# A sparse graph-attention stack: weighted rows in buffers of their own, one-head sums on VectorE

## The chip, the cores and the metric

The kernel runs on one core of one Trainium2 chip. A core has five engines [...]: TensorE (PE, matrix products into PSUM), VectorE (DVE), ScalarE (ACT), GpSimd (POOL, which here issues the gathers and scatters) and SyncE (SP, which issues plain transfers). [...] The metric is the device time of one execution in microseconds (us); it is given as the median of several runs, and the profile is one more execution taken by the hardware profiler.

## The reference, cut to what matters

Four graph-attention layers, each with a layer norm and a ReLU ahead and a residual around it, on 3327 nodes with 512 features. The layers have 8, 4, 1 and 8 heads; layers 1 and 2 end in an ELU.

```python
h = relu(layernorm(x)); v = h @ W                  # 3327 x 512
e[i, j] = leaky_relu(a[i] + b[j], 0.2)             # per head, masked by the adjacency
alpha = softmax(e, axis=j)
out[i] = sum over j of alpha[i, j] * v[j]          # per head
x = x + elu(out)                                   # without elu in layers 0 and 3
```

The adjacency is sparse: a node has 36 neighbours at most, itself included.

## The kernel before: the parts that matter

A first stage (to about 395 us) reads the adjacency, makes for each node a list of its neighbours, sorts the nodes by their number and cuts them into 26 tiles of 128 nodes. Tile t has `CAPS[t]` neighbour places per node, from 36 down to 11, 467 in all. Then each layer runs over the tiles, smallest first, in groups of up to four neighbour places (127 groups). For one place, one gather brings 128 rows of the table `tab` (a projected row of 512 values with its scores, 528 in all), one for each node of the tile.

```python
LOOK = 9
gpool = tile_pool(name="gpool", bufs=LOOK)         # a buffer g holds one group: [128, 4, 528]
...
def fetch(self):                                   # GpSimd: gathers of one group
    g = gpool.tile([P, GROUP, ROW], F32, name="g")
    for q in range(n):
        if l > 0 and k0 + q == 0:
            nc.sync.dma_start(g[:, 0, :], own_d[l % 2][t])        # the node's own row
        else:
            gather(g[:, q, :], tabs[l % 2], idx[:, t, k0 + q:k0 + q + 1])      # L677
...
def scored(self, i):                               # weights of one group
    nc.vector.tensor_tensor(z, g's scores, s, OP.add)                           # L721
    nc.vector.scalar_tensor_tensor(z, z, SLOPE, z, OP.mult, OP.max)             # L723
    nc.scalar.activation(self.wt[:, k0:k0 + n, :H], z, AF.Exp)                  # L724
...
def group(self, i):                                # weight the rows in place, sum them
    for q in range(n):
        v = g[:, q, :] ... [:, :, :F // 2]         # the 512 values, as 2 x 256
        if H == 1:
            nc.scalar.activation(v, v, AF.Copy, scale=wt[:, k0 + q, 0:1])       # L734
        elif q == 3:
            for h in range(H):                     # one activation a head
                nc.scalar.activation(u, u, AF.Copy, scale=wt[:, k0 + q, h:h + 1])  # L738
        else:
            nc.vector.tensor_tensor(v, v, wt broadcast over the head, OP.mult)  # L741
    for q in range(n):                             # sum in PSUM, by the identity
        nc.tensor.matmul(self.po, ident, g[:, q] ..., start=..., stop=...)      # L744
```

When a tile's groups are done, its tail follows in pieces:

```python
def divisors(self):  ...                           # VectorE: 1 / sum of the weights (L750-752)
def means(self):     y = po * den                  # VectorE reads TensorE's sums (L758)
def bent(self):      ...                           # ScalarE, ELU layers only: exp part (L766, L768)
def added(self):     x += y (or its ELU)           # VectorE (L774, L775 or L777), then layer-norm
                     ...                           # statistics and 1/sqrt by Newton steps (L411-L434)
def turn(self):      ...                           # TensorE: four transposes (L444)
def cut(self):       ...                           # ScalarE: ReLU, PSUM to SBUF (L451)
def project(self):   ...                           # TensorE: 8 matmuls with the next W (L462)
def rows(self):      ...                           # ScalarE: scale (L469); SP stores the own rows
def scatter():       ...                           # GpSimd: rows into the next layer's tab (L685)
```

The order of instructions on each engine is that of this loop. Step s fetches groups ahead, scores group s+1, weights and sums group s, and lays the tail's pieces into the following steps:

```python
for s in range(-1, len(steps) + 6):
    while fetched < min(len(steps), s + LOOK): fetch the next group
    do("first"); score group s + 1; do("scored"); weight and sum group s
    if it was the tile's last group:
        late = 1 if ELU[l] else 0
        for d, place, piece in [(0, "last", tl.divisors), (1, "last", tl.means),
                                (2, "scored", tl.bent), (1 + late, "last", tl.added),
                                (2 + late, "first", tl.turn), (2 + late, "scored", tl.cut),
                                (2 + late, "last", tl.project), (3 + late, "scored", tl.rows),
                                (3 + late, "last", scatter)]:
            at.setdefault((s + d, place), []).append(piece)
    do("last")
```

A buffer can be written again when its last reader is done; a gather into g waits for the engine that read g last. Layer l+1 starts gathering when all tiles of layer l are scattered.

Of the kernel before, what the change touches and what calls it, by code (L numbers as in the profile page):

```python
# [20 lines left out]
HEADS = [8, 4, 1, 8]  # L21
SELF = [True, True, False, False]
ELU = [False, True, True, False]
BANK = 512
# [9 lines left out]
GROUP = 4  # L34
# [439 lines left out]
def tile_gat_stack(ctx: ExitStack, tc: tile.TileContext, x, adj, adjT, ws, avs, out):  # L474
# [173 lines left out]
    with cond.Else():  # L648
        tile_gat_lists(tc, x, ws, avs, out, ident, half, idx, tabs, tabs_v)
# [3 lines left out]
def tile_gat_lists(ctx: ExitStack, tc: tile.TileContext, x, ws, avs, out, ident, half, idx, tabs, tabs_v):  # L653

    nc = tc.nc
    NP, F = x.shape
    NT = NP // P
    NL = len(HEADS)

    LOOK = 9  # L660
    xpool = ctx.enter_context(tc.tile_pool(name="xpool", bufs=1))
    wpool = ctx.enter_context(tc.tile_pool(name="wpool", bufs=2))
    gpool = ctx.enter_context(tc.tile_pool(name="gpool", bufs=LOOK))
    spool = ctx.enter_context(tc.tile_pool(name="spool", bufs=3))
# [17 lines left out]
    def scatter():  # L682
        while waiting:
            dst, t, rows = waiting.pop(0)
            nc.gpsimd.indirect_dma_start(out=dst, out_offset=bass.IndirectOffsetOnAxis(ap=ids[t], axis=0),  # L685
                                         in_=rows, in_offset=None)

    class Tile:
# [22 lines left out]
        def scored(self, i):  # L711

            H = HEADS[self.l]
            k0, n, g = self.groups[i]
            if i == 0:
                self.s = small.tile([P, 8], F32, name="s")
                nc.vector.tensor_copy(self.s[:, :H], g[:, 0, F // 2:F // 2 + H])
                self.wt = spool.tile([P, KMAX, 8], F32, name="wt")
                self.po = ps_o.tile([P, BANK], F32, name="po")
            z = small.tile([P, GROUP, 8], F32, name="z")  # L720
            nc.vector.tensor_tensor(z[:, :n, :H], g[:, :n, ROW - 8:ROW - 8 + H],  # L721
                                    self.s[:, :H].unsqueeze(1).to_broadcast([P, n, H]), OP.add)
            nc.vector.scalar_tensor_tensor(z[:, :n, :H], z[:, :n, :H], SLOPE, z[:, :n, :H], OP.mult, OP.max)  # L723
            nc.scalar.activation(self.wt[:, k0:k0 + n, :H], z[:, :n, :H], AF.Exp)  # L724

        def group(self, i):

            H, K, wt = HEADS[self.l], CAPS[self.t], self.wt
            D = F // H
            k0, n, g = self.groups[i]  # L730
            for q in range(n):
                v = g[:, q, :].rearrange("p (s m) -> p s m", s=2)[:, :, :F // 2]
                if H == 1:
                    nc.scalar.activation(v, v, AF.Copy, scale=wt[:, k0 + q, 0:1])  # L734
                elif q == 3:
                    for h in range(H):
                        u = v[:, h * 2 // H, h * D % (F // 2):h * D % (F // 2) + D]
                        nc.scalar.activation(u, u, AF.Copy, scale=wt[:, k0 + q, h:h + 1])  # L738
                else:
                    v = v.rearrange("p s (h d) -> p s h d", d=D)  # L740
                    nc.vector.tensor_tensor(v, v, wt[:, k0 + q, :H].rearrange("p (s h) -> p s h", s=2)  # L741
                                            .unsqueeze(3).to_broadcast([P, 2, H // 2, D]), OP.mult)
            for q in range(n):
                nc.tensor.matmul(self.po, ident, g[:, q, :].rearrange("p (s m) -> p s m", s=2)[:, :, :F // 2],  # L744
                                 start=(k0 + q == 0), stop=(k0 + q == K - 1))

        def divisors(self):
            H, K = HEADS[self.l], CAPS[self.t]
# [3 lines left out]
            nc.vector.reciprocal(den[:, :H], den[:, :H])  # L752

        def means(self):
            H, po, den = HEADS[self.l], self.po, self.den
            D = F // H
            self.y = work.tile([P, F], F32, name="y")
            nc.vector.tensor_tensor(self.y.rearrange("p (h d) -> p h d", h=H),  # L758
                                    po.rearrange("p (h d) -> p h d", h=H),
                                    den[:, :H].unsqueeze(2).to_broadcast([P, H, D]), OP.mult)  # L760

        def bent(self):
# [45 lines left out]
    for l in range(NL):  # L808
        W, following = following, None
        tiles = [Tile(l, t, W) for t in order]  # L810
        steps = [(tl, i) for tl in tiles for i in range(len(tl.k0))]
        at = {}
        fetched = 0
        for s in range(-1, len(steps) + 6):
            def do(place):
                for piece in at.pop((s, place), []):
                    piece()
            while fetched < min(len(steps), s + LOOK):
                steps[fetched][0].fetch()
# [65 lines left out]
```

## Time and profile before

| | |
|---|---|
| time, median of 3 runs | 3442.64 us (3437.56 to 3452.84) |
| profiled execution | 3448.7 us |
| busy: PE, DVE, ACT, POOL | 2380.0, 1690.1, 1111.7, 1990.4 us |
| gathers of rows (L677) | 1790, 1003 ns each |
| products on VectorE (L741) | 1080, 686 ns each |
| weighting by ScalarE in layer 2 (L734) | 467, 712 ns each |
| data moved | 628.25 MB, 182 GB/s on average |

A line of the page's groups names the source line, the engine, the operation, the tile written and those read, the shape, and the count; then the busy time, the mean length of one, and the engine's idle time just before these instructions with what ended most of it. "issue" is idle time for which the profile shows no wait. One matmul of four-byte values shows as two records. GpSimd's record of a gather is the time of its instruction; the data lands after it. The granted clock is the share of full speed that TensorE's throttle let through.

### The profile page before, as it was taken

To read this page: it belongs to the slowest core of one execution; us is meant where nothing else is said; L and a number is where in the kernel's file an instruction comes from. 1 tells how busy PE (TensorE), PEld (TensorE's weight loads), DVE (VectorE), ACT (ScalarE), POOL (GpSimd) and SP (SyncE) were. 2 spreads that over 40 slices of the span, in tenths; PEclk is the share of its full clock that TensorE was granted. 3 is DMA by queue.
4 is the path that set the end of the run, shared out by engine and by line. 5 is a ranking of instruction groups with operands and counts; after the bars stand their busy time and mean duration, and the time that the engine had idled before them with its cause. 6 is when DMAs were issued, how large, how long until landed. Compare 5 with 4: busy or idle time off the path is not lost.

```text
span 3448.7 us, 26822 instructions
## 1 busy us (share of the span) xinstructions
PE 2380.0 (69%) x5830; PEld 1182.6 (34%) x5830; DVE 1690.1 (49%) x4748; ACT 1111.7 (32%) x3431; POOL 1990.4 (58%) x2027
## 2 busy tenths in 40 slices
PE   4554157777777767887777667777777756775766
PEld 2443033333333324443333333333333322332322
DVE  9999246555545446665554323222212145453544
ACT  0111023243333323232322244454454423332433
POOL 1002667666667367676666366556556267777775
PEclk7777578988888879998988889898898878887898
DMA  5552466666666567776666466566666376777675
GB/s 210 205 190 88 126 189 195 200 191 192 189 184 192 138 191 211 199 208 191 197 192 177 117 199 186 171 184 184 177 183 190 88 203 199 204 199 202 197 202 144
DMA packets 197017, 628.25 MB, mean 182 GB/s; under 512 B 38483, under 2 KB 42995, under 8 KB 193525
## 3 DMA queue, kind: packets, MB, share of 16 engines
q0 software_dynamic: 154432, 519.29, 53.7%
q1 hardware_dynamic: 38676, 100.36, 8.4%
q10 hardware_dynamic: 3744, 6.82, 0.5%
q8 instruction: 54, 0.88, 0.1%
q14 instruction: 111, 0.90, 0.1%
HBM read 569.76 MB, written 56.57 MB: 182 GB/s over the span
## 4 chain that ended last, share of the span: by engine, by line
issue 14%; PE 12%; POOL 12%; another core or an unknown queue 11%; DVE 9%; DMA 3%; ACT 3%; POOLq 0%; DVEq 0%; ACTq 0%
POOL g L677 12%; PE po L744 10%; DVE g L741 4%; DMA g<-tab,idx 3%; PE pv L462 2%; ACT g L734 1%; ACT g L738 1%; DVE st L411 1%; DVE x L775 1%; DVE q L432 1%; DVE x L774 1%; DVE z L721 1%; DVE xn L415 1%; POOL tab L685 0%
## 5 line engine op out<-in xcount | busy, mean ns | idle before, releaser
L744 PE MATMUL po<-g,ident 128*128 128x512 f32 x3736 | 1874.0, 658 | 802.3 <-ACT g L738 171.3
L677 POOL DMA_INDIRECT g<-tab,idx x1790 | 1794.7, 1003 | 844.2 <-issue 490.3
L744 PEld LDWEIGHTS po<-g,ident 128*128 128x128 f32 x3736 | 765.1, 210 | 1821.0 <-issue 976.9
L741 DVE TENSOR_TENSOR g<-g,wt 128x512 f32<-128x512 f32 x1080 | 683.1, 686 | 373.9 <-ACT wt L724 217.5
L738 ACT ACTIVATE g<-g,wt 128x64 f32<-128x64 f32 (+1 forms) x2140 | 574.4, 347 | 90.0 <-issue 57.0
L462 PE MATMUL pv<-w,hT 128*128 128x264 f32 x1664 | 458.7, 436 | 26.4 <-ACT hT L451 22.6
L758 DVE TENSOR_TENSOR y<-po,den 128x512 f32<-128x512 f32 x104 | 72.0, 692 | 823.8 <-PE po L744 508.0
L724 ACT ACTIVATE wt<-z 128x32 f32<-128x32 f32 (+7 forms) x508 | 107.7, 215 | 1116.1 <-DVE z L723 360.6
L462 PEld LDWEIGHTS pv<-w,hT 128*128 128x128 f32 x1664 | 360.4, 219 | 146.1 <-issue 36.3
L469 ACT ACTIVATE v<-pv,rstd 128x528 f32<-128x528 f32 x104 | 72.9, 701 | 835.5 <-remote 377.5
L734 ACT ACTIVATE g<-g,wt 128x512 f32<-128x512 f32 x467 | 298.4, 712 | 0.0
L685 POOL DMA_INDIRECT tab<-v,idx x78 | 80.8, 1036 | 241.3 <-ACT v L469 212.7
L444 PE MATMUL pt<-ident,xn 128*128 128x128 f32 x416 | 72.8, 304 | 168.3 <-DVE xn L415 110.8
L721 DVE TENSOR_TENSOR z<-g,s 128x32 f32<-128x32 f32 (+7 forms) x508 | 92.5, 182 | 183.0 <-DMA g<-tab,idx 163.0
L425 POOL TENSOR_TENSOR rstd<-ve,half 128x1 f32<-128x1 f32 x26 | 14.3, 552 | 290.5 <-DVE ve L417 280.4
L451 ACT ACTIVATE hT<-pt 128x512 f32<-128x512 f32 x104 | 61.2, 589 | 245.0 <-PE pt L444 106.3
L546 DVE MAX8 cand<-key 128x8 f32<-128x208 f32 x416 | 135.2, 405 | 0.0
L444 PEld LDWEIGHTS pt<-ident,xn 128*128 128x128 f32 x416 | 54.3, 154 | 223.0 <-issue 149.3
L723 DVE SCALAR_TENSOR_TENSOR z<-z 128x32 f32<-128x32 f32 (+7 forms) x508 | 92.8, 183 | 34.8 <-remote 9.5
L750 DVE TENSOR_REDUCE den<-wt 128x8 f32<-128x120 f32 (+35 forms) x104 | 32.7, 314 | 155.4 <-ACT wt L724 139.3
L541 DVE SCALAR_TENSOR_TENSOR key<-a,keys 128x3328 f32<-128x3328 int32 x26 | 94.5, 3633 | 0.0
L432 DVE TENSOR_SCALAR q<-rstd,hv 128x1 f32<-128x1 f32 x234 | 63.9, 273 | 13.3 <-issue 1.9
(82 smaller groups left out, 759.0 us busy)
## 6 DMA issues: line engine op xcount, KB each, us to landing
a<-in_adj SPq DMA_DIRECT2D x26, 1664.0 KB
g<-tab,idx POOLq DMA_INDIRECT x1790
own<-v SPq DMA_DIRECT2D x78, 264.0 KB
g<-own SPq DMA_DIRECT2D x78, 264.0 KB
tab<-v SPq DMA_DIRECT2D x26, 264.0 KB
xt<-in_x ACTq DMA_DIRECT2D x26, 256.0 KB
w<-in_w SPq DMA_DIRECT2D x8, 512.0 KB
av<-in_a SPq DMA_DIRECT2D x8, 256.0 KB
```

Of the source, the lines that this page charges most:

```text
L432: nc.vector.tensor_scalar(q, rstd, rstd, hv, OP.mult, OP.mult)
L444: nc.tensor.transpose(pt[:, k, :], xn[:, k * P:(k + 1) * P], ident)
L462: nc.tensor.matmul(pv[:, s, :HF + 8], hT[:, k, :], W.w[:, k, s, :], start=(k == 0), stop=(k == KC - 1))
L541: nc.vector.scalar_tensor_tensor(key, a, 0.0, keys, OP.is_gt, OP.mult, accum_out=total[:, t:t + 1])
L546: nc.vector.max(cand[:, g * 8:(g + 1) * 8], key[:, g * SEG:(g + 1) * SEG])
L677: nc.gpsimd.indirect_dma_start(out=out_, out_offset=None, in_=table, in_offset=bass.IndirectOffsetOnAxis(ap=which, axis=0))
L721: nc.vector.tensor_tensor(z[:, :n, :H], g[:, :n, ROW - 8:ROW - 8 + H], self.s[:, :H].unsqueeze(1).to_broadcast([P, n, H]), OP.add)
L724: nc.scalar.activation(self.wt[:, k0:k0 + n, :H], z[:, :n, :H], AF.Exp)
L734: nc.scalar.activation(v, v, AF.Copy, scale=wt[:, k0 + q, 0:1])
L738: nc.scalar.activation(u, u, AF.Copy, scale=wt[:, k0 + q, h:h + 1])
L741: nc.vector.tensor_tensor(v, v, wt[:, k0 + q, :H].rearrange("p (s h) -> p s h", s=2) .unsqueeze(3).to_broadcast([P, 2, H // 2, D]), OP.mult)
L744: nc.tensor.matmul(self.po, ident, g[:, q, :].rearrange("p (s m) -> p s m", s=2)[:, :, :F // 2], start=(k0 + q == 0), stop=(k0 + q == K - 1))
```

## The change

It has four parts, meant to let the engines run past each other:

- the weighted rows of a group go into a buffer m of their own (3 of them), so that a gather buffer is free as soon as it has been weighted; the gathers look 7 instead of 9 groups ahead, which makes room for m;
- in the layer with one head, TensorE and ScalarE no longer weight and sum the rows: VectorE multiplies each row by its weight and adds it to one of two alternating accumulators in SBUF, in one instruction a row;
- the means read TensorE's result two groups after the tile's last group instead of one (with one head, one group after, from the accumulators);
- the later pieces of the tail move back as well: the transposes one step after the residual, the projection one step after those, the rows and the scatter two steps after the projection.

```diff
-    LOOK = 9
+    LOOK = 7
+    apool = ctx.enter_context(tc.tile_pool(name="apool", bufs=2))
+    mpool = ctx.enter_context(tc.tile_pool(name="mpool", bufs=3))
...
-                self.po = ps_o.tile([P, BANK], F32, name="po")
+                if H > 1:
+                    self.po = ps_o.tile([P, BANK], F32, name="po")
... group():
+            if H == 1:
+                if i == 0:
+                    self.acc = apool.tile([P, 2, F], F32, name="acc")
+                for q in range(n):
+                    v = g[:, q, :].rearrange("p (s m) -> p s m", s=2)[:, :, :F // 2]
+                    acc = self.acc[:, (k0 + q) % 2, :].rearrange("p (s m) -> p s m", s=2)
+                    w = wt[:, k0 + q, 0:1]
+                    if k0 + q < 2:
+                        nc.vector.tensor_scalar(acc, v, w, None, OP.mult)
+                    else:
+                        nc.vector.scalar_tensor_tensor(acc, v, w, acc, OP.mult, OP.add)
+                return
+            m = mpool.tile([P, GROUP, F], F32, name="m")
             for q in range(n):
-                if H == 1:
-                    nc.scalar.activation(v, v, AF.Copy, scale=wt[:, k0 + q, 0:1])
-                elif q == 3:
+                if q == 3:
                     for h in range(H):
-                        nc.scalar.activation(u, u, AF.Copy, scale=wt[:, k0 + q, h:h + 1])
+                        nc.scalar.activation(m[:, q, h * D:(h + 1) * D], u, AF.Copy, scale=wt[:, k0 + q, h:h + 1])
                 else:
-                    nc.vector.tensor_tensor(v, v, wt ..., OP.mult)
+                    nc.vector.tensor_tensor(m[:, q, :] ..., v ..., wt ..., OP.mult)
             for q in range(n):
-                nc.tensor.matmul(self.po, ident, g[:, q, :] ..., start=(k0 + q == 0), stop=(k0 + q == K - 1))
+                nc.tensor.matmul(self.po, ident, m[:, q, :], start=(k0 + q == 0), stop=(k0 + q == K - 1))
... means():
+            if H == 1:
+                nc.vector.tensor_add(self.y, self.acc[:, 0, :], self.acc[:, 1, :])
+                nc.vector.tensor_scalar(self.y, self.y, den[:, 0:1], None, OP.mult)
+                return
... the loop:
-        for s in range(-1, len(steps) + 6):
+        for s in range(-1, len(steps) + 9):
-                    late = 1 if ELU[l] else 0
-                    for d, place, piece in [(0, "last", tl.divisors), (1, "last", tl.means),
-                                            (2, "scored", tl.bent), (1 + late, "last", tl.added),
-                                            (2 + late, "first", tl.turn), (2 + late, "scored", tl.cut),
-                                            (2 + late, "last", tl.project), (3 + late, "scored", tl.rows),
-                                            (3 + late, "last", scatter)]:
+                    a = 1 if HEADS[l] == 1 else 2
+                    b = a + 1 if ELU[l] else a
+                    for d, place, piece in [(0, "last", tl.divisors), (a, "last", tl.means),
+                                            (a + 1, "scored", tl.bent), (b, "last", tl.added),
+                                            (b + 1, "first", tl.turn), (b + 2, "scored", tl.cut),
+                                            (b + 2, "last", tl.project), (b + 4, "scored", tl.rows),
+                                            (b + 4, "last", scatter)]:
```

More of the change, by code (lines that the diff above doesn't have):

```diff
@@ L730, in group @@
             k0, n, g = self.groups[i]
+            if H == 1:
[11 more added lines that the diff above has]
+            m = mpool.tile([P, GROUP, F], F32, name="m")
             for q in range(n):
                 v = g[:, q, :].rearrange("p (s m) -> p s m", s=2)[:, :, :F // 2]
-                if H == 1:
-                    nc.scalar.activation(v, v, AF.Copy, scale=wt[:, k0 + q, 0:1])
-                elif q == 3:
+                if q == 3:
                     for h in range(H):
                         u = v[:, h * 2 // H, h * D % (F // 2):h * D % (F // 2) + D]
-                        nc.scalar.activation(u, u, AF.Copy, scale=wt[:, k0 + q, h:h + 1])
+                        nc.scalar.activation(m[:, q, h * D:(h + 1) * D], u, AF.Copy, scale=wt[:, k0 + q, h:h + 1])
                 else:
-                    v = v.rearrange("p s (h d) -> p s h d", d=D)
-                    nc.vector.tensor_tensor(v, v, wt[:, k0 + q, :H].rearrange("p (s h) -> p s h", s=2)
+                    nc.vector.tensor_tensor(m[:, q, :].rearrange("p (s h d) -> p s h d", s=2, d=D),
+                                            v.rearrange("p s (h d) -> p s h d", d=D),
+                                            wt[:, k0 + q, :H].rearrange("p (s h) -> p s h", s=2)
                                             .unsqueeze(3).to_broadcast([P, 2, H // 2, D]), OP.mult)
             for q in range(n):
-                nc.tensor.matmul(self.po, ident, g[:, q, :].rearrange("p (s m) -> p s m", s=2)[:, :, :F // 2],
-                                 start=(k0 + q == 0), stop=(k0 + q == K - 1))
+                nc.tensor.matmul(self.po, ident, m[:, q, :], start=(k0 + q == 0), stop=(k0 + q == K - 1))
         def divisors(self):
@@ L754, in means @@
         def means(self):
-            H, po, den = HEADS[self.l], self.po, self.den
+            H, den = HEADS[self.l], self.den
             D = F // H
             self.y = work.tile([P, F], F32, name="y")
+            if H == 1:
+                nc.vector.tensor_add(self.y, self.acc[:, 0, :], self.acc[:, 1, :])
+                nc.vector.tensor_scalar(self.y, self.y, den[:, 0:1], None, OP.mult)
+                return
             nc.vector.tensor_tensor(self.y.rearrange("p (h d) -> p h d", h=H),
-                                    po.rearrange("p (h d) -> p h d", h=H),
+                                    self.po.rearrange("p (h d) -> p h d", h=H),
                                     den[:, :H].unsqueeze(2).to_broadcast([P, H, D]), OP.mult)
```

## The prediction

> **What bounds the kernel now.** I read the page's busy line first: no engine is full (PE 69%, POOL 58%, DVE 49%, ACT 32% of 3448.7 us). So waits matter, and the next question is who waits for whom. The page's costliest groups (line, engine, operation, tile, count | busy us, mean ns | idle before it and what ended most of it):
>
> ```profile
> L744 PE MATMUL po<-g,ident 128*128 128x512 f32 x3736 | 1874.0, 658 | 802.3 <-ACT g L738 171.3
> L677 POOL DMA_INDIRECT g<-tab,idx x1790 | 1794.7, 1003 | 844.2 <-issue 490.3
> ...
> L758 DVE TENSOR_TENSOR y<-po,den 128x512 f32<-128x512 f32 x104 | 72.0, 692 | 823.8 <-PE po L744 508.0
> ```
>
> The third is the striking one: VectorE stands idle 824 us in front of only 104 instructions, the `means`, mostly until TensorE has finished a tile's sums. The view of waits repeats it and adds that GpSimd's gathers wait for TensorE too, to release a buffer:
>
> ```profile
> DVE y L758 <- PE po L744: 508.0, 74, 23.5
> ...
> POOL g L677 <- PE po L744: 208.5, 96, 11.1
> ```
>
> One tile end in the timeline (start us, length us, engine, line; in brackets the idle time before) shows the ring:
>
> ```profile
> 1000.30 0.95 POOL L677 DMA_INDIRECT g<-tab,idx  x1 [2.78 <-PE po L744]
> ...
> 1004.36 0.69 DVE L758 TENSOR_TENSOR y<-po,den 128x512 f32<-128x512 f32 x1 [5.22 <-PE po L744]
> ...
> 1009.52 1.89 DVE L741 TENSOR_TENSOR g<-g,wt 128x512 f32<-128x512 f32 x3
> 1009.62 1.41 POOL L677 DMA_INDIRECT g<-tab,idx  x1 [0.30 <-DMA g<-tab,idx]
> 1009.64 0.23 ACT L724 ACTIVATE wt<-z 128x32 f32<-128x32 f32 x1 [10.14 <-DVE q L432]
> ...
> 1010.26 5.40 PE L744 MATMUL po<-g,ident 128*128 128x512 f32 x8 [2.08 <-DVE g L741]
> ```
>
> VectorE waits 5.22 us for TensorE; then it does the residual, the statistics and the Newton steps before the next weights and products (1004.36 to 1009.52), and TensorE runs dry behind it. Each engine runs in order, so the two alternate instead of overlapping. Meanwhile a row block is free for the next gather only when TensorE has read it, because it is weighted in place.
>
> The third view is busy time by window, one for each layer's gathers (us of the window, then PE, PEld, DVE, ACT, POOL busy with counts, granted clock, DMA share, GB/s):
>
> ```profile
> 395.00:1160.20 765.20, 559.83 (x1380) 274.01 (x1381) 408.74 (x1076) 241.62 (x972) 525.29 (x517) 0.85 0.68 194
> 1203.00:1899.50 696.50, 522.82 (x1346) 262.62 (x1347) 395.89 (x1056) 193.36 (x613) 463.66 (x457) 0.88 0.69 196
> 1959.40:2690.60 731.20, 525.34 (x1328) 260.38 (x1329) 175.45 (x700) 337.81 (x646) 433.76 (x449) 0.87 0.64 184
> 2763.80:3420.00 656.20, 449.15 (x900) 185.45 (x900) 311.66 (x751) 234.51 (x951) 470.88 (x462) 0.83 0.70 199
> ```
>
> GpSimd's own floor follows from it. When it isn't held, the timeline shows 0.30 us between gathers. A layer has 467 neighbour rows (sum of CAPS); layer 0 gathers all of them and 26 tiles of x, later layers 441 (26 own rows come through SP), and 25 scatters fall inside. With busy/count of the window plus 0.30:
> - layer 0: 518 x (1.016 + 0.30) = 682 us; first to last gather took 766.
> - layer 1: 466 x 1.315 = 613; took 708 (1202.9 to 1910.6).
> - layer 2: 466 x 1.266 = 590; took 752 (1958.1 to 2709.8).
> - layer 3: 466 x 1.319 = 615; took about 660.
>
> So 84 + 95 + 162 + 45 = 386 us are waits of GpSimd inside the layers. TensorE is lower: a matmul record every 0.43 us in the timeline, so a tile of 18 rows costs 36 x 0.43 + 3.7 (projection) + 0.6 (transposes) = 19.8 us against about 23.7 for GpSimd's 18 instructions at 1.315. Between layers GpSimd also stops for the tail:
>
> ```profile
> 1195.11 0.98 POOL L685 DMA_INDIRECT tab<-v,idx  x1 [32.39 <-ACT v L469]
> 1202.93 0.98 POOL L677 DMA_INDIRECT g<-tab,idx  x1 [6.84 <-issue]
> ```
>
> [...]
> - [...] The trace has 692 for `means` and 693 for the existing multiply-adds of 128x512 (L775). I price the new multiply-add with that.
> - [...] counted over all gathers of rows by overlap of start and length, 708 that met no VectorE instruction mean 949 ns and none is over 1000, while 604 that met an L741 product mean 1082 ns; the 1.41 us gather above started 0.1 us into one.
> - [...]
>
> **The change part by part.**
> 1. *Means one step later* (several heads: two groups after the last instead of one). VectorE asks for TensorE's result when TensorE has had one more group's time, 8 x 0.43 = 3.4 us of matmul work stands between, and while VectorE does its 5 us tail TensorE still has two groups to sum. It removes no work, but the 508 us of VectorE waiting and TensorE's drought after each tile. Turn, cut, project and rows also get one step more each.
> 2. *Weighted rows in m (3 buffers), LOOK 9 to 7.* A gather buffer is free after the multiply, not after the matmul; the 208.5 us should nearly vanish. Lookahead falls from 8 groups to 6, still about 6 x 4 x 1.315 = 31 us of gathers, against a VectorE tail of about 7 us. Products cost the same 686 ns.
> 3. *Layer 2 on VectorE.* It removes 467 activations at 712 ns (ScalarE) and 934 matmul records (402 us at 0.43). It adds 467 x 0.69 = 322 us on VectorE plus 26 x (0.69 + 0.55) for adding the two accumulators and dividing, while a 0.69 us `means` goes. VectorE's layer 2: 322 + 46 (127 groups of two z operations at 0.18) + 126 (26 tails of 4.84: two ELU adds, statistics, Newton) + 12 (divisors) + 32 (means) + 15 (own scores, folding) = 553 us.
>    With VectorE that full I let 80% of the gathers meet a two-input operation: 0.8 x 1.08 + 0.2 x 0.95 = 1.055; 441 x 1.355 + 25 x 1.3 = 630 us, 40 more than its floor now. VectorE stands at 553/630 = 88%.
>
> If the waits go, GpSimd sets the pace. The first tiles are the exception: with 11 rows GpSimd needs 10 x 1.315 + 1.3 = 14.4 us, TensorE 22 x 0.43 + 4.3 = 13.8 at full clock, VectorE in layer 2 about 15.4. I add 12 us each for layers 0 and 1, 15 for layer 2 and 10 for layer 3, an allowance. Layers: 694 + 625 + 645 + 625 = 2589.
> Between layers: now 41, 48 and 54 us. At the first one the last matmul ends about 23 us after the last gather, since GpSimd was far ahead; 11 more to the scatter, 8 to the next gather. Consumers close behind GpSimd should need about 12 in place of the 23, with the ELU's extra about 33: 3 x 33 = 99.
> Sum: 395 before the first gather (unchanged) + 2589 + 99 + 24 at the end (3424.9 to 3448.7) = 3107; I say 3110 us, a ratio of 0.903.
>
> **Rivals.**
> - *VectorE becomes the bound in layer 2, or starves the gathers.* For it: 88% full, in order, and gathers that start 0.1 us into a product take about 0.4 us more. If nearly every gather paid 0.25 us, layer 2 would take 441 x 1.5 + 33 = 695. Against it: GpSimd's next gather falls into step with a run of products, and many overlap at 949. Total then about 3160.
> - *The shorter lookahead gives the wait back:* GpSimd held by fewer buffers, a scatter that waits for a later `rows`. Against it: data lands fast, in a stretch of uninterrupted gathers at most two or three gathers are issued and not yet moved. If half of the 386 us stayed: about 3260.
> - *TensorE or its clock becomes the bound.* Its busy time at the granted 0.85 was 560 and 523 us in layers 0 and 1, below 682 and 613; only the small tiles come near. Worth 30 us more.
> - *The transfers are the limit.* Against it: 220 GB/s in an uninterrupted stretch (2080 to 2085) with a DMA share of 0.78, and layer 0 would need 194 x 765/694 = 214.
>
> **Range and chances.** No rival alone brings it near 3443; all waits gone and no allowance would be about 3040. 8 in 10: 3020 to 3240. Faster by over 2%: 0.95; within: 0.04; slower: 0.01.
>
> **What would show it.** Right: the wait of `means` for po under 100 us; gathers waiting for TensorE gone; first-to-last gathers near 694, 625, 645, 625; gather mean in layer 2 near 1.05 us; VectorE over 80% busy there and PE under 25%; gaps between layers near 33. Wrong: gathers that wait for VectorE or ScalarE (the new owner of the buffer) by 100 us and more, a gather mean over 1.15 in layer 2, or VectorE full there with GpSimd idle.

## The result, and the profile after

The changed kernel takes 3341.63 us (median of 4 runs, 3339.68 to 3355.12), the kernel before 3446.51 beside it: a ratio of 0.9706, 95% interval 0.9671 to 0.9741. That is faster, but by 105 us where 333 were predicted. The profiled execution took 3339.0 us.

The page of the changed kernel: the chain that ended last, by engine, and the costliest groups (columns as in the prediction):

```profile
DVE 14%; PE 11%; another core or an unknown queue 11%; issue 11%; POOL 9%; DMA 6%; ACT 2%; DVEq 0%; POOLq 0%; ACTq 0%
...
L679 POOL DMA_INDIRECT g<-tab,idx x1790 | 1829.7, 1022 | 743.1 <-issue 501.3
L760 PE MATMUL po<-m,ident 128*128 128x512 f32 x2802 | 1383.5, 648 | 582.2 <-issue 215.3
L755 DVE TENSOR_TENSOR m<-g,wt 128x512 f32<-128x512 f32 x1080 | 683.6, 686 | 581.7 <-remote 371.2
...
L745 DVE SCALAR_TENSOR_TENSOR acc<-g,wt,acc 128x512 f32<-128x512 f32 x415 | 287.7, 747 | 22.8 <-DVE acc L745 11.0
...
L777 DVE TENSOR_TENSOR y<-po,den 128x512 f32<-128x512 f32 x78 | 53.7, 688 | 120.2 <-PE po L760 89.0
```

The wait of the means has gone as foreseen (824 us of idle time before them are 120 now), yet GpSimd's idle time fell only from 844 to 743 us. The idle time moved: VectorE now stands 582 us before its products, where the kernel before had 374, and the releaser is "remote", something the profile can't name. The same line of the kernel before:

```profile
L741 DVE TENSOR_TENSOR g<-g,wt 128x512 f32<-128x512 f32 x1080 | 683.1, 686 | 373.9 <-ACT wt L724 217.5
```

Waits of the changed kernel (engine, line, waited for: us in total, times, longest):

```profile
DVE m L755 <- remote: 371.2, 38, 18.1
...
ACT v L469 <- remote: 306.2, 22, 26.6
...
ACT m L753 <- remote: 164.2, 16, 17.8
ACT hT L451 <- remote: 137.1, 9, 24.8
...
POOL g L679 <- ACT m L753: 77.5, 35, 10.0
```

Gathers no longer wait for TensorE; they wait for ScalarE and VectorE, the new owners of the buffers, which themselves stand. By layer, the windows from first to last gather (us; PE, PEld, DVE, ACT, POOL busy; granted clock, DMA share, GB/s):

```profile
393.40:1160.10 766.70, 550.73 (x1393) 276.87 (x1394) 412.16 (x1087) 248.07 (x998) 524.60 (x517) 0.85 0.67 194
1197.20:1889.60 692.40, 541.86 (x1381) 268.88 (x1382) 409.50 (x1094) 204.10 (x641) 470.97 (x465) 0.88 0.69 200
1928.60:2605.00 676.40, 178.67 (x500) 130.11 (x500) 479.63 (x1208) 83.48 (x226) 491.45 (x465) 0.60 0.70 205
2636.00:3310.20 674.20, 441.01 (x902) 184.94 (x902) 311.99 (x748) 228.62 (x949) 470.27 (x465) 0.83 0.68 195
```

Against 764.9, 707.6, 751.7 and 659.8 us before, layer 2 gained 75 us and layer 1 15, layers 0 and 3 lost 2 and 14. The gaps between layers fell from 143 to 107 us in all, start and end together changed by less than 1: in sum the 109.7 between the two profiles. Counting every pause of GpSimd beyond its usual 0.30 us, its waits inside the layers went from 85, 96, 163 and 47 us to 88, 82, 46 and 65. Of these, 98 us before and 88 after stand in front of scatters, which wait for ScalarE to write the rows. So the question is why layers 0, 1 and 3 kept theirs.

**A tile end of layer 0.** The timeline of the changed kernel (start, length, engine, line; idle time before in brackets):

```profile
1072.40 2.07 PE L760 MATMUL po<-m,ident 128*128 128x512 f32 x2 [4.22 <-issue]
...
1074.27 5.76 PE L462 MATMUL pv<-w,hT 128*128 128x264 f32 x16
...
1075.47 0.23 ACT L727 ACTIVATE wt<-z 128x32 f32<-128x32 f32 x1 [1.11 <-DVE z L726]
...
1089.55 1.01 PE L760 MATMUL po<-m,ident 128*128 128x512 f32 x1 [2.22 <-issue]
...
1092.34 1.01 PE L760 MATMUL po<-m,ident 128*128 128x512 f32 x1 [1.77 <-issue]
...
1094.45 1.01 PE L760 MATMUL po<-m,ident 128*128 128x512 f32 x1 [1.10 <-issue]
...
1101.52 1.90 DVE L755 TENSOR_TENSOR m<-g,wt 128x512 f32<-128x512 f32 x3 [15.77 <-remote]
...
1102.32 0.70 ACT L469 ACTIVATE v<-pv,rstd 128x528 f32<-128x528 f32 x1 [26.62 <-remote]
...
1103.30 1.00 POOL L687 DMA_INDIRECT tab<-v,idx  x1 [6.07 <-ACT wt L727]
```

TensorE's projection is through at 1080.0 and TensorE goes on with the next sums; ScalarE, which waits for nothing but this projection, starts at 1102.3, 22 us later. GpSimd gathers on at its steady pace until it comes to the scatter of these very rows, which starts at 1103.30, 0.28 us after ScalarE has written them. VectorE's 15.77 us are a late start too: its next product writes the m buffer that TensorE had last read by 1074.47 (first line), and its weights were ready at 1075.70. TensorE's own matmuls meanwhile come only every 2.1 to 2.8 us, and the profile shows no wait for it. Then everything starts at once. In the trace, 10 updates of the semaphore on which TensorE counts its finished work lie between 1101.4 and 1102.6, the last nine 0.04 to 0.06 us apart; the whole trace has 1227 of them, that of the same kernel on a chip without late starts 1687. The ends of matmuls are modelled in the profile, and no record tells when a result could be read; so the trace can't say whether result or count was late. It does say that the next matmuls had started (the first at 1079.86).

I paired each such reader with its producer over the whole trace and took the start minus the later of two ends, the producer's and that of the reader's own preceding instruction. Over 0.3 us, summed (us):

| reader <- producer | before | changed |
|---|---|---|
| ScalarE hT <- TensorE transposes (78) | 105 | 152 |
| ScalarE v <- TensorE projection (78) | 225 | 287 |
| VectorE y <- TensorE sums (104; 78) | 241 | 71 |
| ScalarE weights <- VectorE z (508) | 14 | 17 |
| TensorE projection <- ScalarE hT (78) | 0 | 0 |
| TensorE transposes <- VectorE xn (78) | 1 | 4 |

In these six pairs late starts, up to 22 us, are found practically only where something waits for TensorE. The table is not complete, though. Counted in the same way, the changed kernel's products start late after everything they need, TensorE's last read of their m buffer included: VectorE's by 475 us in all (227 of it in layer 3), ScalarE's by 193 (all in layer 3). The m buffers themselves made this handover. VectorE also starts late on its own results: between instructions that only need the one before (accumulations, statistics, Newton steps and the like) there are 104 us of pauses, 82 of them in layer 2. In the kernel before, VectorE's products start 56 us late after ScalarE's weights. On chip B (below), where the six pairs have no late start, all of these together are one pause of 0.46 us. So late starts are not confined to TensorE's results.

The profile before had them too. In its view of waits they stand among the lines that the prediction quotes, between the 508.0 and the 208.5 us. Its chain that ended last, and these waits:

```profile
issue 14%; PE 12%; POOL 12%; another core or an unknown queue 11%; DVE 9%; DMA 3%; ACT 3%; POOLq 0%; DVEq 0%; ACTq 0%
```

```profile
ACT v L469 <- remote: 377.5, 32, 17.0
...
DVE y L758 <- remote: 241.7, 17, 21.4
```

A one-core program has no other core to wait for; 11% of the chain under that name is 380 us.

### The profile page after: what moved, and what is told of

It is laid out like the page before. It is cut to its first block, busy times and chain, and to the rows that moved or that the text cites. A ratio compares the mean times of both kernels' runs of the same rounds, so it can differ in the third digit from the quotient of the medians.

```text
span 3339.0 us, 23138 instructions
## 1 busy us (share of the span) xinstructions
PE 1968.0 (59%) x4896; PEld 1030.7 (31%) x4896; DVE 1995.3 (60%) x5241; ACT 828.7 (25%) x2964; POOL 2026.2 (61%) x2027
## 4 chain that ended last, share of the span: by engine, by line
DVE 14%; PE 11%; another core or an unknown queue 11%; issue 11%; POOL 9%; DMA 6%; ACT 2%; DVEq 0%; POOLq 0%; ACTq 0%
PE po L760 9%; POOL g L679 9%; DMA g<-tab,idx 5%; DVE m L755 4%; DVE acc L745 3%; PE pv L462 2%; ACT m L753 1%; DVE z L724 1%; DVE q L432 1%; DVE st L411 1%; DVE x L794 1%; DVE x L793 1%; DVE z L726 1%; DVE rstd L434 1%
## 5 line engine op out<-in xcount | busy, mean ns | idle before, releaser
L679 POOL DMA_INDIRECT g<-tab,idx x1790 | 1829.7, 1022 | 743.1 <-issue 501.3
L760 PE MATMUL po<-m,ident 128*128 128x512 f32 x2802 | 1383.5, 648 | 582.2 <-issue 215.3
L755 DVE TENSOR_TENSOR m<-g,wt 128x512 f32<-128x512 f32 x1080 | 683.6, 686 | 581.7 <-remote 371.2
L760 PEld LDWEIGHTS po<-m,ident 128*128 128x128 f32 x2802 | 568.0, 208 | 1327.2 <-issue 803.3
L462 PE MATMUL pv<-w,hT 128*128 128x264 f32 x1664 | 524.2, 482 | 232.0 <-ACT hT L451 173.2
L753 ACT ACTIVATE m<-g,wt 128x64 f32<-128x64 f32 (+1 forms) x2140 | 565.0, 345 | 205.9 <-remote 164.2
L462 PEld LDWEIGHTS pv<-w,hT 128*128 128x128 f32 x1664 | 401.7, 246 | 369.3 <-ACT hT L451 191.2
L745 DVE SCALAR_TENSOR_TENSOR acc<-g,wt,acc 128x512 f32<-128x512 f32 x415 | 287.7, 747 | 22.8 <-DVE acc L745 11.0
L777 DVE TENSOR_TENSOR y<-po,den 128x512 f32<-128x512 f32 x78 | 53.7, 688 | 120.2 <-PE po L760 89.0
L793 DVE SCALAR_TENSOR_TENSOR x<-ex,x 128x512 f32<-128x512 f32 x52 | 35.9, 691 | 135.2 <-ACT ex L787 113.6
```

What stands on the lines that cost most here:

```text
L462: nc.tensor.matmul(pv[:, s, :HF + 8], hT[:, k, :], W.w[:, k, s, :], start=(k == 0), stop=(k == KC - 1))
L679: nc.gpsimd.indirect_dma_start(out=out_, out_offset=None, in_=table, in_offset=bass.IndirectOffsetOnAxis(ap=which, axis=0))
L745: nc.vector.scalar_tensor_tensor(acc, v, w, acc, OP.mult, OP.add)
L753: nc.scalar.activation(m[:, q, h * D:(h + 1) * D], u, AF.Copy, scale=wt[:, k0 + q, h:h + 1])
L755: nc.vector.tensor_tensor(m[:, q, :].rearrange("p (s h d) -> p s h d", s=2, d=D), v.rearrange("p s (h d) -> p s h d", d=D), wt[:, k0 + q, ...
L760: nc.tensor.matmul(self.po, ident, m[:, q, :], start=(k0 + q == 0), stop=(k0 + q == K - 1))
```

## The experiments

The theory at the start: TensorE's results reach their readers late as long as gathers run unbroken. Rival A, from the prediction: the shorter lookahead gives the waits back. Rival B: TensorE is the bound. The runs were placed on five chips, called A to E here; each is compared with the kernel before on the same chip.

| run | chip | us | before there | ratio, 95% interval |
|---|---|---|---|---|
| later reading alone | A | 3027.05 | 3040.02 | 0.9962 (0.9948 to 0.9976) |
| one-head part alone | A | 3068.08 | 3040.02 | 1.0098 (1.0081 to 1.0115) |
| m buffers, LOOK 7 alone | A | 3051.50 | 3040.02 | 1.0038 (1.0024 to 1.0053) |
| changed kernel, LOOK 5 | A | 3072.97 | 3040.02 | 1.0109 (1.0092 to 1.0126) |
| kernel before | B | 3039.87 | 3039.62 | one execution |
| changed kernel | B | 3065.02 | 3039.62 | 1.0092 (1.0075 to 1.0109) |
| changed, layer 2 undone | B | 3022.56 | 3039.62 | 0.9939 (0.9920 to 0.9958) |
| one-head part, again | C | 3060.41 | 3036.98 | 1.0081 (1.0055 to 1.0107) |
| later reading, again | C | 3020.08 | 3036.98 | 0.9940 (0.9918 to 0.9961) |

The kernel before takes 3037 to 3040 us on A, B and C, 3448 and 3441 on D and E, and 3443 in the first runs, whose chip the records don't name. The chip is the great variable of this case.

**Parts alone (chip A).** Later reading, in place, 9 groups ahead:

```diff
-                    late = 1 if ELU[l] else 0
-                    for d, place, piece in [(0, "last", tl.divisors), (1, "last", tl.means), ...
+                    a = 2
+                    b = a + 1 if ELU[l] else a
+                    for d, place, piece in [(0, "last", tl.divisors), (a, "last", tl.means), ... as in the change
```

> The kernel before with only the later reading (means two groups after the tile's last group in all four layers, transposes, projection, rows and scatter later as in the change); rows still weighted in place, 9 groups ahead, layer 2 still on ScalarE and TensorE. Theory (TensorE's results reach their waiters late, 5 to 20 us after TensorE is done, as long as gathers run unbroken, so the engines stop all the same until the gathers have run out of buffers): the wait of the means for po falls from 508 us to under 200, but the waits of ScalarE and VectorE labelled remote grow, and the time falls by 0 to 50 us only. Rival A (the lookahead of 7 groups gives the wait back): with 9 groups kept, this part alone brings 80 us and more. Rival B (TensorE is the bound of layers 0, 1 and 3): within 20 us of the kernel before.

The one-head layer on VectorE, all else as before:

```diff
+            if H == 1:
+                ... multiply-add into acc, as in the change, LOOK = 9
+                return
```

> The kernel before with only the one-head layer changed (VectorE multiplies each row and adds it to one of two accumulators); in-place weighting elsewhere, 9 groups ahead, means and tail where they were. Theory: layer 2 then asks TensorE only for transposes and projections; its 752 us fall to about 690 and the time falls by 60 to 75 us, most of what the whole change brought. Rival A: 30 to 70 us. Rival B (TensorE the bound): layer 2 loses its bound, 75 us and more, and the other layers stay the same to 10 us.

The buffers alone; layer 2 is weighted by ScalarE into m:

```diff
-    LOOK = 9
+    LOOK = 7
+            m = mpool.tile([P, GROUP, F], F32, name="m")
-                    nc.scalar.activation(v, v, AF.Copy, scale=wt[:, k0 + q, 0:1])
+                    nc.scalar.activation(m[:, q, :] ..., v, AF.Copy, scale=wt[:, k0 + q, 0:1])
```

> The kernel before with only the buffers changed (weighted rows in m, three of them; 7 groups ahead instead of 9), layer 2 weighted by ScalarE into m, means and tail where they were. Theory: the gathers' 208 us wait for TensorE goes, but the engines that free the gather buffers stop for the late results as before; within 40 us of the kernel before on either side. Rival A (lookahead): slower by 30 us or more. Rival B: no change beyond 15 us.

The changed kernel with a shorter lookahead:

```diff
-    LOOK = 7
+    LOOK = 5
```

> The changed kernel with 5 instead of 7 groups ahead. Theory (late results under unbroken gathers): gathers run out of buffers sooner, the stops come sooner and are shorter; the time is within 30 us of the changed kernel's 3342, the remote waits of ScalarE and VectorE shrink. Rival A (lookahead too short): 60 us slower or more, the gathers' waits inside layers 0, 1 and 3 grow from 235 us to 300 and more. Rival B (TensorE the bound): no change beyond 15 us.

Measured: 3027, 3068, 3052 and 3073 us. All four expectations were written for a kernel of 3443 us and none could be judged as meant, for here the kernel before took 3040. The traces show why: not one late start of the six pairs in any of them, and GpSimd's waits inside the layers are 9, 9, 33 and 9 us in all. The layers lie on the floors that the prediction had worked out for GpSimd (682, 613, 590 and 615): 677, 617, 591 and 615 us with the later reading alone. The theory's condition falls as well: here gathers run unbroken for 600 us and more, and nothing comes late.

**Both kernels, unchanged, on a chip without late starts (B).**

> The kernel before, unchanged, once more with a profile. In the runs of its parts it took 3040 us in place of the 3443 of the first profile, and their traces have no wait labelled remote on ScalarE's reading of the projections. Theory (the 386 us of GpSimd's waits were late arrivals of TensorE's completion counts, not the order of the instructions): where ScalarE starts on a projection within 0.3 us of its end, the layers lie at GpSimd's own floors of 682, 613, 590 and 615 us to 5%, and the time is near 3040; where ScalarE starts 5 us and more late at many tiles, it is near 3440. Rival (the order of the instructions makes the waits): the layers are as long as in the first profile even where ScalarE is never late.

> The changed kernel, unchanged, against the kernel before on the same chip. Theory: if TensorE's results come without delay here, the layers of both are GpSimd's floor and the change can only cost: layer 2 goes from about 600 to 630 us (longer gathers beside VectorE's multiply-adds); total 3050 to 3085, slower by 0.3 to 1.5%. If the results come late as in the first profiles, 2 to 4% faster again. Rival (order and lookahead): about 100 us faster in either case.

Measured: 3039.87 and 3065.02 us; both as the theory had it. The kernel before by layer on chip B:

```profile
396.70:1077.70 681.00, 555.74 (x1410) 267.91 (x1410) 412.34 (x1084) 253.01 (x1007) 524.15 (x517) 0.93 0.77 218
1110.90:1727.50 616.60, 532.80 (x1410) 266.69 (x1410) 410.99 (x1092) 203.16 (x641) 475.13 (x465) 0.94 0.77 224
1763.10:2365.60 602.50, 505.37 (x1394) 256.03 (x1395) 181.88 (x727) 351.15 (x674) 449.85 (x465) 0.98 0.79 230
2402.40:3014.50 612.10, 455.69 (x910) 181.83 (x910) 313.11 (x752) 230.80 (x957) 470.64 (x465) 0.91 0.75 214
```

With nearly the busy times that GpSimd had in the first profile (525, 473, 449 and 474 us there by layer) the layers are 84, 91, 149 and 48 us shorter. Its waits show what the order of the instructions really cost:

```profile
ACT v L469 <- PE pv L462: 573.9, 101, 8.6
...
DVE y L758 <- PE po L744: 299.5, 48, 13.0
```

VectorE still waits 300 us for the sums and ScalarE 574 for the projections, and GpSimd, 8 groups ahead, isn't held by either: 20 us in all four layers. That is a wait that costs nothing. The same tile end as above, in the changed kernel on chip B:

```profile
987.34 3.72 PE L462 MATMUL pv<-w,hT 128*128 128x264 f32 x16
...
990.90 3.60 PE L760 MATMUL po<-m,ident 128*128 128x512 f32 x8
...
995.51 0.68 ACT L469 ACTIVATE v<-pv,rstd 128x528 f32<-128x528 f32 x1
```

ScalarE reaches the projection 4.5 us after its end and starts without a pause; TensorE's eight records take 0.45 us each, where they stood 2.1 us apart. And layer 2, the only one that the change alters here:

```profile
1752.70:2386.40 633.70, 180.95 (x500) 131.51 (x500) 478.14 (x1205) 82.11 (x225) 492.33 (x465) 0.60 0.76 218
```

31 us longer than before (602.5): the gathers there average 1.053 us in place of 0.965, GpSimd is busy 492.3 us in place of 449.9, and 11 us of waits went.

**Layer 2 undone (B).**

```diff
-            if H == 1:
-                ... multiply-add into acc ...
+                if H == 1:
+                    nc.scalar.activation(m[:, q, :] ..., v, AF.Copy, scale=wt[:, k0 + q, 0:1])
```

> The changed kernel with its layer 2 undone: ScalarE weights the rows into m and TensorE sums them; m buffers, 7 groups ahead and the later tail stay. Theory, results without delay: layer 2 back at a gather mean of 0.97 us and about 600 us, total 3020 to 3045, within 1% of the kernel before and faster than the changed kernel by 20 us and more. Results late: layer 2 keeps most of its 752 us, and the total is 3380 to 3440, only the gaps between layers gained. Rival (order): 60 us and more faster than before in either case.

Measured: 3022.56; layer 2 at 591 us with gathers of 0.966. Where results come at once, the one-head part is what costs, and the rest gains 0.6%.

**Late starts put in by hand.** If late starts make the 386 us, then putting them into a kernel on a chip that has none must make it slow. For each tile whose hT, v or y started more than 0.3 us late in the first profile, the reader first copies TensorE's result into a spare buffer for as long; the copies wait for TensorE as the reader does. Nothing is left out.

```diff
+                for _ in range(round(LATE["v"].get((self.l, self.t), 0) / 0.6)):
+                    nc.scalar.activation(idle_a, self.pv[:, :, :ROW // 2], AF.Copy)
                 v = scaled(nc, self.pv, self.rstd, work)
```

and likewise ahead of hT (ScalarE, 0.55 us each) and of y (VectorE, 0.62). The first four ran on chip D, where results come late by themselves (kernel before: 3448), so that these were added to those.

> The kernel before with the late starts of its first profile put in by hand, tile by tile: where ScalarE or VectorE there began on a finished TensorE result (transposes, projection, sums) 0.3 us or more too late, it now first copies that result into a spare buffer for as long (571 us in all over 90 of 260 handovers: 105 on the transposes, 225 on the projections, 241 on the sums). Nothing is left out. Theory (these late starts, not the order of the instructions, made GpSimd's 386 us of waits in the first profile): the time goes from 3040 to 3200 or more, towards 3443, and GpSimd's waits inside the layers from under 25 us to 150 and more. Rival (the lookahead of 9 groups absorbs such stops; the 386 us came from something else, such as TensorE's own slow stretches): under 3110.

> The changed kernel with the late starts of its own first profile put in the same way (509 us in all over 71 of 234 handovers: 151, 287, 71). Theory: from 3065 to 3200 and more, towards 3342, with GpSimd's waits back in layers 0 and 1 above all (late starts there 108 and 141 us on the projections alone). Rival: under 3130.

> The changed kernel with the late starts of the kernel before's profile (553 us; those on layer 2's sums fall away, since VectorE sums there). Theory: the later reading does not take away a stop that begins only when TensorE is done, so this costs nearly what it cost the kernel before outside layer 2; with layer 2 less dependent on TensorE the time lies 30 to 120 us below that of the kernel before with the same late starts. Rival (later reading hides late results): within 40 us of the 3065 without them.

> The changed kernel with layer 2 back on ScalarE and TensorE, and the late starts of the kernel before's profile (571 us). Theory: buffers and later tail alone give back little of the stops; within 60 us of the kernel before with the same late starts, above the changed kernel with them. Rival: within 40 us of the 3023 without them.

Measured: 3862.63, 3680.90, 3579.96 and 3709.55. The absolute figures of the expectations hold for a chip without late starts. Two differences can be judged all the same, and both were missed: against the kernel before with the same late starts, the changed kernel lies 283 us lower (30 to 120 expected), the one with layer 2 undone 153 lower (within 60 expected). Then chip C, which has none:

> The one-head part alone once more, on whichever chip comes. Theory: where TensorE's results come late (kernel before near 3443), this part alone brings most of the change's gain, 60 to 110 us (ratio 0.970 to 0.983), all of it in layer 2; where they come at once (kernel before near 3040), it costs 20 to 30 us again. Rival (the gain of 105 us came from the later reading): within 30 us of the kernel before where results come late.

> The later reading alone once more. Theory: where results come late, within 40 us of the kernel before (a stop that begins when TensorE is done isn't hidden by reading one step later); where they come at once, 10 to 20 us faster again. Rival: 60 us and more faster where results come late.

> The kernel before with the late starts of its first profile put in by hand (571 us). On a chip where results come late anyway this cost 414 us. Theory: on a chip where they come at once, 3200 and more, 160 us and more above the kernel before, with GpSimd's waits inside the layers at 150 us and more. Rival (the stops that were put in only cost on top of others): under 3110.

> The changed kernel with its own late starts (509 us), which cost 340 us on top of a late chip. Theory: 3180 and more on a chip where results come at once; rival: under 3130.

The parts alone repeated what chip A gave. The kernel before with 571 us of late starts took 3410.74 us, 374 above the 3037 there; the first profile took 3449, 38 more. In the trace the copies took 606 us (226 on the projections, 111 on the transposes, 269 on the sums), 6% more than the late starts that they stand for. The gathers kept their lengths: 1020, 1011, 963 and 1017 ns by layer, where chip B has 1009, 1020, 965 and 1010. By layer (first to last gather; pauses beyond 0.30 us):

| | layer 0 | 1 | 2 | 3 | gaps | waits |
|---|---|---|---|---|---|---|
| before, first profile | 764.9 | 707.6 | 751.7 | 659.8 | 41.5, 47.6, 54.0 | 391 |
| before, chip B | 681.0 | 616.5 | 602.4 | 612.1 | 33.2, 35.6, 36.8 | 20 |
| before with late starts, chip C | 749.8 | 714.6 | 750.9 | 632.6 | 39.4, 48.1, 54.3 | 355 |
| changed, first profile | 766.7 | 692.4 | 676.4 | 674.2 | 37.0, 39.0, 31.0 | 281 |
| changed, chip B | 676.3 | 616.2 | 633.7 | 612.8 | 32.8, 33.4, 31.6 | 9 |
| changed with its late starts, chip C | 770.4 | 685.9 | 634.8 | 615.5 | 37.5, 35.7, 33.1 | 166 |

The match goes down to the waits that the prediction was built on. In the kernel before with late starts put in:

```profile
DVE y L766 <- PE po L750: 544.6, 73, 23.4
...
POOL g L680 <- PE po L750: 248.1, 170, 11.6
```

Those were 508.0 and 208.5 us in the first profile. The mean granted clock came along: 0.848, where the first profile had 0.845 and the kernel before on the same chip C 0.901 to 0.910 in ten executions. Nothing but stops of ScalarE and VectorE was added, so the lower clock here came of TensorE being kept waiting and needs no cause of its own (Rival B). In the changed kernel the late starts give layers 0 and 1 their length again, to 7 us, and leave layers 2 and 3 where chip B has them. Its total is 3232.01 us of 3342: some 100 us of layers 2 and 3 are not explained by them. The first profile points to the late starts that were not put in. In layer 3, ten of GpSimd's twelve pauses over 0.7 us end with a product into m, and these products start late there by 227 us on VectorE and 193 on ScalarE; in layer 2 VectorE pauses 82 us between its own instructions. No run puts these in, so this part is argued, not shown.

**Which part makes the kernel less sensitive (chips D and E).** The same late starts (the kernel before's) in each variant; both chips are late by themselves, with the kernel before at 3448 and 3441.

> The changed kernel with the late starts of the kernel before's profile (553 us), once more, beside the two parts alone. With 3411 us for the kernel before with these starts where nothing else is late, and the gap of 283 us seen between the two on the late chip: 3130 to 3250. Theory: most of that gap is layer 2, so this lies 60 us and more below the later reading alone with the same late starts. Rival: as low as the later reading alone, to 40 us.

> The later reading alone with the late starts of the kernel before's profile (571 us). Theory: it reads later, but a stop put in begins when the engine gets there, so only its looser coupling helps: 40 to 120 us below the 3411 of the kernel before with them (where nothing else is late). Rival (the later reading is what makes the change robust): 200 us and more below.

> The one-head part alone with the late starts of the kernel before's profile (553 us). Theory: layer 2 falls from 751 to about 640 us, the other layers stay at 750, 715 and 633; 90 to 130 us below the 3411 of the kernel before with them. Rival: 50 us below or less.

| with the kernel before's late starts | chip | us | layers 0 to 3 | waits |
|---|---|---|---|---|
| kernel before | D | 3862.63 | 848, 828, 857, 739 | 790 |
| one-head part alone | E | 3658.04 | 854, 828, 691, 735 | 582 |
| later reading alone, 9 groups, in place | E | 3484.53 | 761, 730, 756, 670 | 426 |
| changed, layer 2 undone (later, m, 7 groups) | D | 3709.55 | 796, 818, 814, 734 | 674 |
| changed kernel | D, E | 3579.96, 3536.40 | 818, 811, 675, 758 (D) | 533 |

On E the changed kernel's figure is that of the faster of two executions; the other took 3595.88.

The theory missed here. It gave the later reading alone 40 to 120 us, and that is 378 us below the kernel before; it put the changed kernel 60 us and more below the later reading alone, and that lies 52 above. The one-head part brings 205 us, more than the 90 to 130 expected, 166 of it in layer 2.

Most of what the later reading saves is one wait, that of GpSimd in front of scatters inside the layers: 293 us in the kernel before, 32 with the later reading alone. In the fourth row, with m and 7 groups in place of 9, it is 295 again, and 225 of the 378 us are lost. The prediction had named such "a scatter that waits for a later `rows`" under the shorter lookahead. But m and the 7 groups were only changed together, and m brings late starts of its own (409 us in that trace, VectorE and ScalarE together), so which of the two loses the 225 us is not shown. D and E are also two chips; the kernel before and the changed kernel differ by under 2% between them. On A, where nothing is late, lookahead is worth little: 5 groups cost 8 us against 7 (3073 on A, 3065 on B).

No version was run on D or E without added late starts, except the kernel before. The later reading alone with them is only 43 us above the kernel before without, so it is the one to try there; where results come at once it beats both kernels (0.994 to 0.996, against 1.009 for the change).

## Why the prediction was wrong

The step that failed is the one from parts 1 and 2 to the sum: that the 386 us in which GpSimd stood still inside the layers were made by the order of the instructions and the in-place buffers, and so would vanish with "If the waits go, GpSimd sets the pace". Nearly all of them were made by late starts on finished results, 571 us of them on TensorE's. On a chip without late starts the same instructions in the same order have 20 us of such waits; with stops at these places put in by hand they have 355 of the 391. That each engine works in order was not the error: in the profile before, the records of the four layers begin in the order of the loop without an exception, 5296 on TensorE, 3756 on VectorE, 3375 on ScalarE and 1920 on GpSimd.

- *Means later, 508 us:* the wait went (89 us plus 24 labelled remote). But on chip B the kernel before waits 300 us for po and loses nothing by it. So the waiting for po was not the cost in itself; the late starts that the order passed on were.
- *Buffers, 208.5 us:* the gathers' wait for TensorE went, and came back as waits for ScalarE and VectorE (77.5 for L753, 53.5 for the weights, 33.5 for z), since both started late themselves. "Wrong: gathers that wait for VectorE or ScalarE" was the sign I had named.
- *Layer 2 on VectorE:* right in kind. Gather mean 1.056 us (1.055 predicted); 676 us (645 predicted), and 634 on chip B. The multiply-add was mis-sized: 747 ns, not 690, so 415 x 0.057 = 24 us more. The price was an estimate from operations that the profile before has (692 ns for `means`, 693 for the multiply-adds with a constant, L775); the measurement decides. VectorE was nevertheless 71% busy, not 88% (479.6 of 676.4). I had added up the lengths of its instructions; these do sum to 532 us in that window, near my 553, but the instructions overlap and keep VectorE busy for 479.6. On chip B it was not the bound: GpSimd waits 2 us in that layer.
- *Layers and gaps:* predicted 694, 625, 645, 625 and three times 33. On chip B the changed kernel has 676, 616, 634, 613 and 33, 33, 32. The floors and gaps were sound, the allowances some 50 us too wide; total 3065 against 3110. (My floor without allowances was mis-added: 3107 less 49 is 3058, not 3040.) What was wrong is that the starting point, 3443, contained a cost that the change for the most part doesn't remove.
- *Rivals:* the shorter lookahead, put at 3260, was never varied alone where results are late. Its sign, GpSimd waiting before a scatter, is there (88 us), but the kernel before has it too (98). TensorE's clock followed the stops on chip C, as told above.

## What to carry to other kernels

A wait labelled "remote" or "another core" in a one-core program isn't noise: pair readers and producers and look for starts that come long after the producer's end, before you charge the waits behind them to the schedule. Run the kernel before on a second chip before a wait of hundreds of us is explained, and put the stops in by hand to see what they are worth. An engine that is far enough ahead hides long waits of the others: on chip B GpSimd stands 20 us in its layers while ScalarE waits 574. Whether lookahead that looks idle on a prompt chip is needed on a late one stays open here.

## What the hardware showed that I had not expected

- The same kernel differs by 13% between chips (3037 to 3040 us on three, 3441 and 3448 on two), and the sign of the change with it: 0.971 in the first comparison, 1.009 on chip B.
- The first profiles hold fewer semaphore updates than those from chip B. For the kernel before, TensorE's counter has 1493 in the first profile and 2148 on chip B, VectorE's 2285 and 4278, ScalarE's 1314 and 2302, and each of the eight counters of the gathers' transfers 1133 to 1297 in place of 3890 or more. No run here tests whether this and the late starts have one cause; why two chips are late stays open.
- A VectorE multiply-add with a scalar from SBUF took 746 to 747 ns on average at 512 elements (the changed kernel's first profile and chip B, the one-head part on chip A), 733 at the least in the first of these; the same operation with a constant (the residual, L794 there) took 692. The two differ in their rows too (the former reads them as 2 x 256), so the reason isn't separated.
